# One float32r pass for item 0 ahead of the count, halves, and two PSUM tiles for v in a recurrent scoring kernel

## The chip, the cores and the metric

The kernel runs on one core of a Trainium2 chip. The metric is the device time of one execution in microseconds (us), the median of several. PE is the matmul engine, DVE VectorE, ACT ScalarE, POOL GpSimd, SP SyncE; PSUM is the memory that takes the matmuls' results. Every run is timed beside the kernel before on the same chip.

## The reference, condensed to what matters

```python
emb = emb_table.at[0].set(0.0)              # 100001 x 128
e = emb[seq]                                # 1024 x 50 x 128
prefix = jnp.cumsum(e, axis=1)
uF = prefix / minimum(t + 1, lengths)
y = batchnorm(uF, over the 1024 sequences) * gamma + beta
def step(v, x):                             # 50 steps
    v = v + (x - v) / 2
    spike = v >= 1
    return v - spike, spike
scores = mean(spikes) @ emb.T               # 1024 x 100001, 409.6 MB
```

## The kernel before

Stage one makes 50 steps; stage two multiplies the spike counts with the table and stores the scores. Row 0 of the table (item 0) counts as zeros, but the gathers fetch the row as it is stored; what is called the pass takes it off again. A step of stage one, cut:

```python
# POOL: eight gathers of 128 rows for step t + 1; three tiles e in turn
for n in range(NB):
    nc.gpsimd.indirect_dma_start(out=es[t][:, n * P : (n + 1) * P], ...)
# PE: transposes add the rows to the running sum pre (PSUM)
for n in range(NB):
    nc.tensor.matmul(pre[:, n * P : (n + 1) * P], lhsT=e[...], rhs=ident, is_transpose=True, ...)
for h in range(B // BANK):                      # DVE: statistics
    nc.vector.scalar_tensor_tensor(uF[:, cs], rlen[:, cs], 1.0 / (t + 1), pre[:, cs], ...)
    nc.vector.bn_stats(bs[:, h, :], uF[:, cs])
...
if t:
    spike(t - 1, 0, B)                          # DVE
    nc.vector.tensor_tensor(negv, s, v, ALU.subtract)
    counted(t - 1, s, 0, B)                     # PE, bf16
if not last:
    correct(t + 1, l)                           # PE: "the pass", takes item 0 off pre, FP32
...                                             # DVE: coefficient a
v = ps(2, f"v_{t}")                             # one PSUM tile for v
nc.scalar.activation(v[:, cs], uF[:, cs], AF.Identity, bias=hgb[:, 1:2], scale=a)
nc.vector.scalar_tensor_tensor(v[:, cs], negv[:, cs], -0.5, v[:, cs], ALU.mult, ALU.add)
```

## Time and profile before

| | before |
|---|---|
| timed runs | 1740.95 to 1741.6 us, median 1741.49 |
| the execution that the profile shows | 1716.87 us, span 1715.1 us |
| step of stage one | 11.07 us |
| first store of scores | 591.94 us |
| stage two | 1123 us |

The lines behind this stand in the prediction.

### The profile page before, as it was taken

The page shows a single profiled execution, that of the slowest core. Times are in us where ns is not written, and L with a number is a line of the kernel's source. Part 1 is how long each engine was busy: PE and PEld are TensorE (multiplying, and loading weights), DVE is VectorE, ACT ScalarE, POOL GpSimd, SP SyncE. Part 2 cuts the span into 40 slices and gives each one's busy share as a digit, 9 for nine tenths or more (in the row PEclk, how much of TensorE's full clock was granted, in tenths as well). Part 3 has the DMA queues.
Part 4 walks back from the last instruction along what each step waited for, and adds up shares of the span by engine and source line. Part 5 has one row for each costly group of instructions (what it writes and reads, how often), then busy time and mean ns, then how long its engine had stood idle before and what let it go on. Part 6 is the DMA issues. An engine that isn't in the chain of part 4 may idle for free.

```text
span 1715.1 us, 13957 instructions
## 1 busy us (share of the span) xinstructions
PE 1260.2 (73%) x4614; PEld 837.6 (49%) x4626; DVE 972.8 (57%) x1257; ACT 635.8 (37%) x697; POOL 378.8 (22%) x406
## 2 busy tenths in 40 slices
PE   4555666555565677887788777887778788888886
PEld 1222222222232365665566655666556666666664
DVE  5666666666666644554545545455445555555554
ACT  2222222222222334444434444444344444444443
POOL 7777666766665000000000000000000000000000
PEclk9999999999985589999999999999999999999999
DMA  9811111111111199999999999999999999999998
GB/s 267 241 52 50 47 48 49 48 48 48 47 44 37 71 392 398 395 405 394 387 395 395 401 393 393 394 393 402 393 395 390 397 415 409 403 404 405 403 403 348
DMA packets 97920, 488.71 MB, mean 285 GB/s; under 512 B 14821, under 2 KB 16568, under 8 KB 48696
## 3 DMA queue, kind: packets, MB, share of 16 engines
q1 hardware_dynamic: 85048, 461.59, 69.1%
q0 software_dynamic: 12800, 26.24, 5.4%
q8 instruction: 36, 0.59, 0.1%
q14 instruction: 36, 0.29, 0.1%
HBM read 78.17 MB, written 409.60 MB: 284 GB/s over the span
## 4 chain that ended last, share of the span: by engine, by line
DMA 48%; PE 29%; DVE 18%; ACT 2%; issue 2%; POOL 0%; DVEq 0%; ACTq 0%; SPq 0%
DMA scores<-o 48%; PE pre L175 11%; PE po L295 10%; PE pre L208 5%; DVE o L303 5%; DVE bs L224 4%; DVE uF L221 4%; DVE s L198 3%; PE count L186 3%; ACT o L305 2%; DVE mv L226 1%; PE pt L95 0%; POOL e L125 0%; DVE nm L232 0%; DVE lo L97 0%
## 5 line engine op out<-in xcount | busy, mean ns | idle before, releaser
L295 PE MATMUL po<-hi,countR 128*128 128x512 f32 x1568 | 681.6, 435 | 182.9 <-DVE o L303 181.6
L303 DVE TENSOR_SCALAR o<-po 128x1024 f32<-128x1024 f32 x392 | 479.0, 1222 | 459.7 <-DMA scores<-o 372.0
L295 PE MATMUL po<-lo,countR 128*128 128x512 f32 x1568 | 646.5, 413 | 0.0
L305 ACT ACTIVATE o<-po 128x1024 f32<-128x1024 f32 (+1 forms) x392 | 399.7, 1020 | 633.8 <-DMA scores<-o 394.0
L295 PEld LDWEIGHTS po<-hi,countR 128*128 128x128 f32 x1568 | 314.3, 200 | 341.9 <-DVE o L303 266.9
L125 POOL DMA_INDIRECT e<-in_L_rec_emb_table,idx x400 | 378.1, 945 | 171.5 <-issue 100.7
L295 PEld LDWEIGHTS po<-lo,countR 128*128 128x128 f32 x1568 | 315.3, 201 | 58.3
L186 PE MATMUL count<-s,ident_h 128*128 128x512 bf16 x88 | 45.6, 605 | 225.0 <-DVE s L198 225.0
L175 PE MATMUL pre<-zT,l 50*128 50x512 f32 x200 | 188.9, 1097 | 10.4 <-issue 4.3
L97 DVE TENSOR_TENSOR lo<-pt,hi 128x1024 fp32r<-128x1024 f32 x98 | 119.6, 1221 | 84.8 <-ACT hi L96 84.8
L186 PEld LDWEIGHTS <-ident_h 128*128 128x128 bf16 x100 | 12.6, 126 | 238.0 <-issue 238.0
L230 ACT ACTIVATE r<-mv,eps 128x1 f32<-128x1 f32 x50 | 14.7, 295 | 290.4 <-DVE mv L226 290.4
L221 DVE SCALAR_TENSOR_TENSOR uF<-rlen,pre 128x512 f32<-128x512 f32 x100 | 67.8, 678 | 88.1 <-PE pre L208 88.1
L95 PE MATMUL pt<-ident,rows 128*128 128x128 f32 x782 | 108.2, 282 | 11.2 <-DVE o L303 10.3
L208 PEld LDWEIGHTS pre<-ident,e 128*128 128x128 f32 x400 | 79.0, 224 | 69.2 <-issue 67.7
L95 PEld LDWEIGHTS pt<-ident,rows 128*128 128x128 f32 x782 | 89.4, 144 | 45.3 <-DVE o L303 34.1
L175 PEld LDWEIGHTS pre<-zT,l 50*128 50x128 f32 x200 | 58.3, 321 | 99.0 <-issue 95.2
L96 ACT CAST hi<-pt 128x1024 fp32r<-128x1024 f32 x98 | 98.5, 1005 | 12.0 <-PE pt L95 12.0
L259 ACT ACTIVATE v<-uF,hgb,a 128x1024 f32<-128x1024 f32 (+1 forms) x51 | 60.7, 1190 | 111.4 <-DVE a L251 111.2
L262 DVE SCALAR_TENSOR_TENSOR v<-negv,v 128x1024 f32<-128x1024 f32 (+1 forms) x51 | 61.6, 1208 | 67.5 <-ACT v L259 67.4
L208 PE MATMUL pre<-ident,e 128*128 128x128 f32 x400 | 98.1, 426 | 0.0
L224 DVE BATCH_NORM_STATS2 bs<-uF 128x6 f32<-128x512 f32 x100 | 69.4, 694 | 3.4
(36 smaller groups left out, 284.1 us busy)
## 6 DMA issues: line engine op xcount, KB each, us to landing
scores<-o SPq DMA_DIRECT2D x384, 1024.0 KB, 9.0
scores<-o SPq DMA_DIRECT2D x8, 848.5 KB, 7.4
e<-in_L_rec_emb_table,idx POOLq DMA_INDIRECT x400, 2.5
rows<-in_L_rec_emb_table SPq DMA_DIRECT2D x1, 832.0 KB
rows<-in_L_rec_emb_table SPq DMA_DIRECT2D x48, 0.5 KB, 11.7
len_i<-in_r_lengths SPq DMA_DIRECT2D x1, 512.0 KB, 4.8
idx<-in_r_seq SPq DMA_DIRECT2D x1, 200.0 KB, 2.8
r<-in_L_rec_emb_table SPq DMA_DIRECT2D x1, 25.0 KB
```

What stands on the lines that cost most here:

```text
L95: nc.tensor.transpose(pt[:, k0 : k0 + kw], r[:kw, (h0 + k0) // P, :], ident[:kw, :kw])
L96: nc.scalar.copy(hi[:, :hw], pt[:, :hw])
L97: nc.vector.tensor_tensor(lo[:, :hw], pt[:, :hw], hi[:, :hw].bitcast(F32), ALU.subtract)
L125: nc.gpsimd.indirect_dma_start(out=es[t][:, n * P : (n + 1) * P], out_offset=None, in_=table, in_offset=bass.IndirectOffsetOnAxis(ap=idx[: ...
L175: nc.tensor.matmul(pre[:, h * BANK : (h + 1) * BANK], lhsT=l, rhs=zT[:, h * BANK : (h + 1) * BANK], start=t == 0, stop=False, skip_group_c ...
L186: nc.tensor.matmul(count[:, c : c + BANK], lhsT=ident_h, rhs=s[:, c : c + BANK], start=t == 0, stop=t == T - 1, skip_group_check=True,)
L208: nc.tensor.matmul(pre[:, n * P : (n + 1) * P], lhsT=e[:, n * P : (n + 1) * P], rhs=ident, start=False, stop=last, is_transpose=True, skip ...
L221: nc.vector.scalar_tensor_tensor(uF[:, cs], rlen[:, cs], 1.0 / (t + 1), pre[:, cs], ALU.max, ALU.mult)
L224: nc.vector.bn_stats(bs[:, h, :], uF[:, cs])
L295: nc.tensor.matmul(po[:, k0 : k0 + kw], lhsT=countR[:, n * P : (n + 1) * P], rhs=part[:, k0 : k0 + kw], start=j == 0, stop=j == 1,)
L303: nc.vector.tensor_scalar_mul(o[:, h0 : h0 + hw], po[:, :hw], 1.0 / T)
L305: nc.scalar.mul(o[:, h0 : h0 + hw], po[:, :hw], 1.0 / T)
```

## The change

Its intent: make the pass cheap (one float32r matmul per half, 128 rows deep, the upper rows carrying the remainder of row 0), take it and the count out of the ring of waits, and let DVE work on one half while PE transposes the other. Cut to its core (the preparation of zT and row 0 for the float32r pass, the division of the last step into halves and new pools are left out):

```diff
-            for n in range(NB):
-                nc.tensor.matmul(pre[:, n * P : (n + 1) * P], ..., is_transpose=True)
-            for h in range(B // BANK):
-                nc.vector.scalar_tensor_tensor(uF[:, cs], rlen[:, cs], ..., pre[:, cs], ...)
+            for h, cs in enumerate(halves):
+                for k in range(0, BANK, P):
+                    nc.tensor.matmul(pre[h][:, k : k + P], ..., is_transpose=True)
+                nc.vector.scalar_tensor_tensor(uF[:, cs], rlen[:, cs], ..., pre[h], ...)
                 nc.vector.bn_stats(bs[:, h, :], uF[:, cs])
+            if not last:
+                correct(t + 1, l)
...
             if t:
-                spike(t - 1, 0, B)
-                nc.vector.tensor_tensor(negv, s, v, ALU.subtract)
-                counted(t - 1, s, 0, B)
-            if not last:
-                correct(t + 1, l)
+                if not last:
+                    spike(s, v, whole)
+                for h in range(len(halves)):
+                    counted(t - 1, s, h)
...
-            l = sp.tile([T, D], F32, tag="l", name=f"l_{t}")
+            l = sp.tile([P, D], F32R, tag="l", name=f"l_{t}")
...
-            v = ps(2, f"v_{t}")
+            vt = vp.tile([P, B], F32, tag=f"v{t % 2}", name=f"v_{t}")
```

More of the change, by code (lines that the diff above doesn't have):

```diff
@@ L44, in rec_kernel @@
     NB = B // P
-    assert D == P and B == HALF and T <= P
+    assert D == P and B == HALF and T <= P // 2
     ctx.enter_context(tc.manual_schedule())
     const = ctx.enter_context(tc.tile_pool(name="const", bufs=1))
-    psum = ctx.enter_context(tc.tile_pool(name="psum", bufs=1, space=bass.MemoryType.PSUM))
     embp = ctx.enter_context(tc.tile_pool(name="embT", bufs=4))
     rowp = ctx.enter_context(tc.tile_pool(name="rows", bufs=AHEAD))
-    def ps(i, name):
-        return psum.tile([P, HALF], F32, tag=f"ps{i % 4}", name=name)
     countR = const.tile([P, B], F32R, tag="countR", name="countR")
@@ L77, in fetch, with prepare @@
         rows[c0] = r
-    def prepare(c0, h0, slot):
+    def prepare(c0, h0, pt):
         w = min(CH, N - c0)
@@ L91, in prepare @@
             nc.vector.memset(lo[:, hw : hw + 1].bitcast(F32), 0.0)
-        pt = ps(slot, f"pt_{c0}_{h0}")
         for k0 in range(0, hw, P):
@@ L106, in rec_kernel @@
         lp = ph.enter_context(tc.tile_pool(name="lif", bufs=2))
+        accp = ph.enter_context(tc.tile_pool(name="acc", bufs=1, space=bass.MemoryType.PSUM))
+        vp = ph.enter_context(tc.tile_pool(name="v", bufs=1, space=bass.MemoryType.PSUM))
         idx = once.tile([P, NB, T], I32, tag="idx", name="idx")
@@ L111, in rec_kernel @@
         nc.sync.dma_start(out=len_i, in_=lengths.rearrange("(o b) -> o b", o=1).to_broadcast([P, B]))
-        r0 = once.tile([T, D], F32, tag="r0", name="r0")
-        nc.sync.dma_start(out=r0, in_=table[0:1, :].to_broadcast([T, D]))
+        r0 = once.tile([P, D], F32, tag="r0", name="r0")
+        nc.sync.dma_start(out=r0, in_=table[0:1, :].to_broadcast([P, D]))
         gb = once.tile([P, 2], F32, tag="gb", name="gb")
@@ L135, in rec_kernel @@
         nc.vector.tensor_copy(ident_h, ident)
-        isz = gp.tile([P, NB, T], F32, tag="e", name="isz")
-        nc.vector.tensor_single_scalar(
-            isz.rearrange("p n t -> p (n t)"), idx.rearrange("p n t -> p (n t)"), 0.0, ALU.is_equal
-        )
-        zps = ps(3, "zps")
-        for n in range(NB):
-            nc.tensor.transpose(zps[:T, n * P : (n + 1) * P], isz[:, n, :], ident)
-        zT = once.tile([T, B], F32, tag="zT", name="zT")
-        nc.vector.tensor_copy(zT, zps[:T, :])
-        r0n = once.tile([T, D], F32, tag="r0n", name="r0n")
-        nc.vector.tensor_scalar_mul(r0n, r0, -1.0)
+        isz = gp.tile([P, NB, P], F32, tag="e", name="isz")
+        nc.vector.memset(isz, 0.0)
+        for u in (0, P // 2):
+            nc.vector.tensor_single_scalar(isz[:, :, u : u + T], idx, 0.0, ALU.is_equal)
+        zps = vp.tile([P, B], F32, tag="v1", name="zps")
+        for n in range(NB):
+            nc.tensor.transpose(zps[:, n * P : (n + 1) * P], isz[:, n, :], ident)
+        zT = once.tile([P, B], F32R, tag="zT", name="zT")
+        nc.vector.tensor_copy(zT, zps)
+        r0hi = once.tile([P, D], F32R, tag="r0hi", name="r0hi")
+        nc.scalar.copy(r0hi, r0)
+        r0n = once.tile([P, D], F32, tag="r0n", name="r0n")
+        nc.vector.tensor_scalar_mul(r0n, r0hi.bitcast(F32), -1.0)
+        up2 = slice(P // 2, P)
+        nc.vector.tensor_tensor(r0n[up2, :], r0hi[up2, :].bitcast(F32), r0[up2, :], ALU.subtract)
+        sel = once.tile([P, P // 2], F32, tag="sel", name="sel")
+        nc.vector.tensor_tensor(sel, ident[:, : P // 2], ident[:, P // 2 :], ALU.add)
         rlen = once.tile([P, B], F32, tag="rlen", name="rlen")
@@ L161, in rec_kernel @@
         nc.vector.memset(negv, 0.0)
-        pre = ps(0, "pre")
-        count = ps(1, "count")
+        pre = [accp.tile([P, BANK], F32, tag=f"pre{h}", name=f"pre{h}") for h in range(B // BANK)]
+        count = [accp.tile([P, BANK], F32, tag=f"count{h}", name=f"count{h}") for h in range(B // BANK)]
         def row0(t):
-            l = sp.tile([T, D], F32, tag="l", name=f"l_{t}")
-            nc.scalar.activation(l, r0n, AF.Copy, scale=ident[:T, t : t + 1])
+            l = sp.tile([P, D], F32R, tag="l", name=f"l_{t}")
+            nc.scalar.activation(l, r0n, AF.Copy, scale=sel[:, t : t + 1])
             return l
@@ L175, in correct @@
                 nc.tensor.matmul(
-                    pre[:, h * BANK : (h + 1) * BANK],
+                    pre[h],
                     lhsT=l,
@@ L182, in correct, with counted, spike @@
                 )
-        def counted(t, s, b0, b1):
-            for c in range(b0, b1, BANK):
-                nc.tensor.matmul(
-                    count[:, c : c + BANK],
-                    lhsT=ident_h,
-                    rhs=s[:, c : c + BANK],
-                    start=t == 0,
-                    stop=t == T - 1,
-                    skip_group_check=True,
-                )
+        def counted(t, s, h):
+            nc.tensor.matmul(
+                count[h],
+                lhsT=ident_h,
+                rhs=s[:, h * BANK : (h + 1) * BANK],
+                start=t == 0,
+                stop=t == T - 1,
+                skip_group_check=True,
+            )
+        def spike(s, v, cs):
+            nc.vector.tensor_single_scalar(s[:, cs], v[:, cs], V_TH, ALU.is_ge)
+        whole = slice(0, B)
+        halves = [slice(h * BANK, (h + 1) * BANK) for h in range(B // BANK)]
         v = s = None
-        def spike(t, b0, b1):
-            nc.vector.tensor_single_scalar(s[:, b0:b1], v[:, b0:b1], V_TH, ALU.is_ge)
         correct(0, row0(0))
@@ L206, in rec_kernel @@
             e = es.pop(t)
-            for n in range(NB):
-                nc.tensor.matmul(
-                    pre[:, n * P : (n + 1) * P],
-                    lhsT=e[:, n * P : (n + 1) * P],
-                    rhs=ident,
-                    start=False,
-                    stop=last,
-                    is_transpose=True,
-                    skip_group_check=True,
-                )
+            if last:
+                spike(s, v, whole)
+                nc.vector.tensor_tensor(negv, s, v, ALU.subtract)
             uF = up.tile([P, B], F32, tag="uF", name=f"uF_{t}")
             bs = sp.tile([P, B // BANK, 6], F32, tag="bs", name=f"bs_{t}")
-            for h in range(B // BANK):
-                cs = slice(h * BANK, (h + 1) * BANK)
-                nc.vector.scalar_tensor_tensor(
-                    uF[:, cs], rlen[:, cs], 1.0 / (t + 1), pre[:, cs], ALU.max, ALU.mult
-                )
+            for h, cs in enumerate(halves):
+                for k in range(0, BANK, P):
+                    nc.tensor.matmul(
+                        pre[h][:, k : k + P],
+                        lhsT=e[:, h * BANK + k : h * BANK + k + P],
+                        rhs=ident,
+                        start=False,
+                        stop=last,
+                        is_transpose=True,
+                        skip_group_check=True,
+                    )
+                nc.vector.scalar_tensor_tensor(uF[:, cs], rlen[:, cs], 1.0 / (t + 1), pre[h], ALU.max, ALU.mult)
                 nc.vector.bn_stats(bs[:, h, :], uF[:, cs])
+            if not last:
+                correct(t + 1, l)
             mv = sp.tile([P, 2], F32, tag="mv", name=f"mv_{t}")
@@ L238, in rec_kernel @@
             if t:
-                spike(t - 1, 0, B)
-                nc.vector.tensor_tensor(negv, s, v, ALU.subtract)
-                counted(t - 1, s, 0, B)
-            if not last:
-                correct(t + 1, l)
+                if not last:
+                    spike(s, v, whole)
+                for h in range(len(halves)):
+                    counted(t - 1, s, h)
             nc.vector.reciprocal(r, r)
@@ L251, in rec_kernel @@
             nc.vector.tensor_scalar(a, r, hgb[:, 0:1], None, ALU.mult)
-            v = ps(2, f"v_{t}")
-            s = lp.tile([P, B], BF16, tag="s", name=f"s_{t}")
-            step = BANK if last else B
-            for b0 in range(0, B, step):
-                cs = slice(b0, b0 + step)
-                nc.scalar.activation(v[:, cs], uF[:, cs], AF.Identity, bias=hgb[:, 1:2], scale=a)
-            for b0 in range(0, B, step):
-                cs = slice(b0, b0 + step)
-                nc.vector.scalar_tensor_tensor(v[:, cs], negv[:, cs], -0.5, v[:, cs], ALU.mult, ALU.add)
-                if last:
-                    spike(t, b0, b0 + step)
-                    counted(t, s, b0, b0 + step)
+            vt = vp.tile([P, B], F32, tag=f"v{t % 2}", name=f"v_{t}")
@@ new lines, in rec_kernel @@
+            st = lp.tile([P, B], BF16, tag="s", name=f"s_{t}")
+            for h, cs in enumerate(halves if last else [whole]):
+                nc.scalar.activation(vt[:, cs], uF[:, cs], AF.Identity, bias=hgb[:, 1:2], scale=a)
+                if t and not last:
+                    nc.vector.tensor_tensor(negv, s, v, ALU.subtract)
+                nc.vector.scalar_tensor_tensor(vt[:, cs], negv[:, cs], -0.5, vt[:, cs], ALU.mult, ALU.add)
+                if last:
+                    spike(st, vt, cs)
+                    counted(t, st, h)
+                    for k in range(0, BANK, P):
+                        put = nc.scalar.copy if k % (2 * P) == 0 else nc.vector.tensor_copy
+                        put(countR[:, h * BANK + k : h * BANK + k + P], count[h][:, k : k + P])
@@ L266, in rec_kernel @@
+            v, s = vt, st
             if t + 2 < T:
                 l = row0(t + 2)
-            if T - 8 <= t < T - 4:
-                prepare((t - T + 8) // 2 * CH, t % 2 * HALF, 3)
-        for n in range(NB):
-            cs = slice(n * P, (n + 1) * P)
-            if n % 2 == 0:
-                nc.scalar.copy(countR[:, cs], count[:, cs])
-            else:
-                nc.vector.tensor_copy(countR[:, cs], count[:, cs])
+            if T - 10 <= t < T - 2 and t % 2 == 0:
+                k = (t - T + 10) // 2
+                prepare(k // 2 * CH, k % 2 * HALF, vp.tile([P, HALF], F32, tag="v1", name=f"pt_{k}"))
@@ L280, in rec_kernel @@
     op = ctx.enter_context(tc.tile_pool(name="o", bufs=4, reuse_waits="tile"))
-    turn = slot = 0
+    psum = ctx.enter_context(
+        tc.tile_pool(name="psum", bufs=4, space=bass.MemoryType.PSUM, reuse_waits="tile")
+    )
+    turn = 0
     for c0 in range(0, N, CH):
@@ L288, in rec_kernel @@
                 hw = min(HALF, w - h0)
-                po = ps(slot, f"po_{c0}_{n}_{h0}")
-                slot += 1
+                po = psum.tile([P, HALF], F32, tag="ps", name=f"po_{c0}_{n}_{h0}")
                 for k0 in range(0, hw, BANK):
@@ L311, in rec_kernel @@
                 if nxt + h0 < N:
-                    prepare(nxt, h0, slot)
-                    slot += 1
+                    prepare(nxt, h0, psum.tile([P, HALF], F32, tag="ps", name=f"pt_{nxt}_{h0}"))
             if n == 4 and c0 + AHEAD * CH < N:
```

## The prediction

> **What bounds the kernel now.** I read the page's slices first, then the windows, then one step of the first stage in the chain of waits and the timeline, and last the waits of the engine that seemed unimportant. In the slices the DMA share is 1 tenth from the third slice to the fourteenth and 9 tenths after it, so there are two stages. In the timeline the first store of scores is issued at 591.94 us and the span ends at 1715.1 us. The windows (start:end, length, then busy time of PE, PEld, DVE, ACT, POOL; granted clock, DMA share, GB/s) show what each stage is short of:
>
> ```profile
> 200.00:300.00 100.00, 59.11 (x126) 26.75 (x126) 67.01 (x136) 25.81 (x36) 67.90 (x72) 1.00 0.17 48
> 300.00:400.00 100.00, 58.87 (x124) 26.75 (x126) 67.29 (x136) 25.81 (x36) 68.24 (x73) 1.00 0.17 48
> ...
> 700.00:1715.00 1015.00, 830.09 (x3502) 609.05 (x3502) 529.29 (x441) 437.14 (x439) 0.00 (x0) 0.95 1.00 396
> ```
>
> Stage two is DMA at a share of 1.00 and 396 GB/s. The change does not alter its bytes, so I take its 1715.1 - 591.9 = 1123 us as fixed: what matters is when the first store leaves. In stage one no engine is busy over 70%, so it must be a chain, here one step of it (start, us, what):
>
> ```profile
> 302.63 0.22 DVE mv L226
> 302.88 0.15 DVE nm L232
> 303.03 0.06 DVE ve L235
> 303.10 1.14 DVE s L198
> 304.24 0.04 issue
> 304.28 1.01 PE count L186 x2
> 305.29 3.71 PE pre L175 x4
> 309.00 1.92 PE pre L208 x8
> 310.94 0.70 DVE uF L221
> ```
>
> The reader is to see a ring: statistics (2.8 us), aggregation, spike, count, the 3.71 us pass that takes item 0 off, eight transposes, and again statistics at 310.94. The one before began at 299.87: a step is 11.07 us. The pass sits behind the count in PE's order, the count behind the spike; so PE's 6.7 us lie in series with 4.4 us of DVE. The timeline shows DVE idle 1.99 us before each uF, waiting for the transposes.
>
> The reader should also look at POOL, which gathers the embeddings, eight gathers in a step:
>
> ```profile
> 304.28 0.10 PEld L186 LDWEIGHTS <-ident_h 128*128 128x128 bf16 x1 [4.72 <-issue]
> 305.11 0.94 POOL L125 DMA_INDIRECT e<-in_L_rec_emb_table,idx  x1 [0.30 <-issue]
> ...
> 306.36 0.94 POOL L125 DMA_INDIRECT e<-in_L_rec_emb_table,idx  x1 [0.31 <-issue]
> ...
> 307.61 0.95 POOL L125 DMA_INDIRECT e<-in_L_rec_emb_table,idx  x1 [0.30 <-issue]
> ```
>
> ```profile
> POOL e L125 <- issue: 100.7, 330, 0.6
> POOL e L125 <- PE pre L208: 58.3, 39, 3.7
> ```
>
> They start 1.25 us apart, 0.94 us of work and a gap of 0.30 us for which nothing is named (330 times). Eight are 10.0 us of the 11.07. The remaining wait, 58.3 us in 39 steps, is for a gather buffer that the transposes free. POOL's 68% busy hides an engine that can go at most 10% faster: the gap belongs to its period.
>
> [...] four FP32 instructions over 512 columns are 3.71 us for both halves, against a start distance of 0.43 us for a float32r matmul of 512 columns at the start of stage two (586 to 592 us)[...]. [...] here 0.944 us stand against a median of 2.5 us from issue to landing. [...] the gathers last 938/944/1438 ns (least/median/most), one of them at 1.44 us in the prologue and otherwise steady beside a DVE that is 67% busy[...].
>
> **The change, part by part.** (1) The pass becomes one float32r matmul for each half, 128 rows deep (upper rows carry the remainder of row 0): 2 x 0.43 = 0.9 us, call it 1.1 with its loads, so 2.6 us less PE work. (2) It moves in front of the count and needs only the uF operations that read its half, so PE does transposes, pass, count, and then the next step's transposes without waiting for DVE's later work: the order of instructions of the changed kernel shows this, each transpose waiting only for its own gather. PE's 1.97 + 1.1 + 1.0 = 4.1 us leave the ring. (3) With two PSUM tiles for v, the subtraction for negv (1.2 us) moves from before the coefficient a to the time in which ACT computes v (1.21 us). DVE's chain then is, with starts read from the step at 299.87: statistics, aggregation and spike 4.39 us; reciprocal to a, 1.04 us; ACT's v with negv beside it, 1.26 us; the update of v, 1.25 us; together 7.9 to 8.0 us. If DVE set the pace, 11.07 would become 8.0.
>
> (4) It does not: the gathers need 8 x 1.25 = 10.0 us in a step. POOL begins at 3.78 us and is not held in front: its third tile needs the first transposes, which by my count end at about 23.5 us (zeroed isz tile, two comparisons and the split of row 0 delay the prologue by some 2 us, the shorter pass gives 2.7 back), while POOL comes to it at 25.0. Step t of DVE would start at 28.5 + 8t, its last gather lands at about 16 + 10t; from t = 6 on POOL sets the pace. In the trace before, the 33rd gather starts at 44.98; 367 more at 1.25 give 503.7, plus 2.5 for landing 506.2 us.
>
> (5) The end: one transpose and the second half's uF and bn (about 508.4; the first half waits for spike and negv of the step before, which costs half a us), aggregation 0.25, coefficient 1.4, first half of v on ACT 0.8, update, spike 1.4, count 0.6, four copies of 0.31 to countR, then update, spike, count of the second half 2.0: 516.2 us for the first product, for which the two counts stand ahead on PE. Before it was 586.52. The 5.4 us from there to the first store stay, so 521.6 against 591.9: 70 us less. Of these some 53 are the pace (50 x 1.07), 9 the four prepared tiles (2.2 us of each was in the ring, now in POOL's shadow, as 8.0 + 1.7 is under 10), the rest the prologue that POOL has already overlapped and the shorter end. Stage two is unchanged but for its pool of four PSUM tiles, used in the same turn.
>
> Timed runs are longer than the profiled span (1741.49 against 1715.1); I take the 26 us over. 1741.5 - 70.3 = 1671 us, 4.0% less.
>
> **The rivals.** (a) DVE sets the pace and the gathers keep up: 50 x 8.0 + 28.5 + 12 would put the first store near 445, some 147 us less, 1594 us. For it, POOL looks only 68% busy; against it, the gap of 0.30 us appears 330 times, also in the first 25 us where no buffer is awaited. I think this the trap in the change. (b) The ring closes elsewhere: the transposes of the tile being prepared need a v tile, v must wait for it, and DVE waits on copies in the last step. At 3 us for each of four tiles 12 us are lost: 1683 us. [...] (d) The time saved is lost in stage two: it would need under 373 GB/s instead of 396; nothing in the diff does that.
>
> **Range and chances.** POOL's rate is measured on 400 instructions, and 0.02 us on the period is 8 us; prologue and end are good to 5 us; (b) and (c) lie above, and only (a) below. So 1658 to 1688 us, eight times in ten. Faster by 2% means under 1706.7 us, half of my gain: 0.95. Within 2%: 0.04. Slower: 0.01.
>
> **What would show it right or wrong.** Right: steps 10.0 us apart; POOL's wait for the transposes gone and its starts 1.25 us apart to the end; PE or DVE waiting for gathers in most steps; the pass at 0.4 to 0.6 us for each half; DVE about 80% busy in the middle of the stage; the last gather at about 504 us; first store at about 522; 1123 us after it. A step of 8 us would mean that the gap of 0.30 us is not part of POOL's period; over 10.3, that a wait that I have not seen entered the ring; a first store at 522 without the gain, that stage two was slowed.

The forecast's sum is 1741.5 - 70.3 = 1671 us. Rival (c): a denser DVE slows the gathers, by a guessed share. The paragraph before "The change, part by part" compares measured times: the pass's four FP32 records are 3.71 us, matmuls of float32r in a row start 0.43 us apart (at a granted clock of 0.50, `--windows 586:592`), and a gather's record is 0.944 us where it lands after 2.5.

## The result, and the profile after

The changed kernel took 1725.22 us (1723.19 to 1726.24, four runs) against 1741.22 us of the kernel before in the same rounds. The ratio is 0.9907, 95% interval 0.9889 to 0.9924: the same within 2%. I had expected 0.96.

The windows of its profiled execution (1723.19 us), in the columns that the prediction explains:

```profile
200.00:300.00 100.00, 36.65 (x104) 21.76 (x104) 64.58 (x134) 24.89 (x36) 67.14 (x71) 0.53 0.16 47
...
700.00:1640.00 940.00, 776.91 (x3269) 576.02 (x3267) 492.78 (x409) 409.46 (x409) 0.00 (x0) 0.94 1.01 398
```

Stage two is as before (share 1.01, 398 GB/s). In stage one POOL makes 71 gathers in 100 us where before it made 72, and the granted clock (third number from the end) has fallen from 1.00 to 0.53. The first store leaves at 598.5 us, later than the 591.94 of before. The chain of waits shows where the time is (start, us, what):

```profile
112.69 1.12 DVE negv L266
...
114.02 1.23 DVE v L267
115.25 7.52 another core or an unknown queue
122.77 0.02 issue
122.79 0.69 DVE uF L228
...
124.21 2.85 another core or an unknown queue
127.06 0.69 DVE uF L228
```

DVE is done at 115.25 and waits 7.5 us and then 2.9 us for something that the profile cannot name. Such a stall comes in every third step: the other two take 7.74 us, the third 18.3, together 33.8 us or 11.27 us a step (the mean of steps 10 to 40). POOL's waits (line, releaser: us in total, times, longest) and the statistics' group:

```profile
POOL e L122 <- issue: 109.3, 358, 0.6
POOL e L122 <- remote: 64.4, 16, 5.4
```

```profile
L228 DVE SCALAR_TENSOR_TENSOR uF<-rlen,pre 128x512 f32<-128x512 f32 x100 | 67.9, 679 | 144.8 <-remote 129.3 <-issue 14.7 <-PE pre L219 0.7
```

POOL's wait for the transposes (58.3 us before) is gone by name, but 64.4 us of "remote", in 16 waits, stand in its place; DVE's wait before uF is "remote" as well. This is a kernel on one core: nothing remote exists in it. The timeline around the stall (start, us, instruction, in brackets the idle time before it):

```profile
112.60 1.91 PE L219 MATMUL pre<-ident,e 128*128 128x128 f32 x8
...
122.79 0.69 DVE L228 SCALAR_TENSOR_TENSOR uF<-rlen,pre 128x512 f32<-128x512 f32 x1 [7.54 <-remote]
...
127.05 0.69 DVE L228 SCALAR_TENSOR_TENSOR uF<-rlen,pre 128x512 f32<-128x512 f32 x1 [2.84 <-remote]
127.29 0.95 POOL L122 DMA_INDIRECT e<-in_L_rec_emb_table,idx  x1 [4.09 <-remote]
```

The eight transposes that DVE and POOL wait for start at 112.60 and look finished at 114.51. The records of PE's semaphore updates say otherwise. These are us after the step's first transpose, read from the trace: the first number of the stalled step is the count's update, the next eight are the transposes'.

```
stalled step, at 112.60:  0.36 | 2.46 5.26 7.36 10.17 12.96 14.36 14.40 14.43
prompt step,  at 130.95:  0.22 | 0.43 0.64 0.86 1.07 (two missing) 1.71 1.92
```

The fourth transpose's update comes at 122.77, and uF starts at 122.79; the eighth comes at 127.03, and the second uF starts at 127.05. So these late updates are what everybody waited for. Their gaps are multiples of 0.70 us (2.10, 2.80, 2.10, 2.81, 2.79, 1.40), and the last three arrive 0.03 us apart, faster than PE can transpose (its starts are 0.21 us apart). Hence PE had done the work, and the news of it was late. Only PE's news was: in the same stretch a VectorE update is recorded at 127.75, 0.01 us after its uF ends, and updates of gathers' transfers are recorded at 114.46, 115.73 and 116.94, some 2.2 us after those gathers start. Whether PE's writes to PSUM were still awaited or only the updates were held up, the trace does not say. The rows were there too: the last packet of this step's gathers ends at 104.40 us. The matmuls' records do not show this: the eight look finished at 114.51, and the last update comes at 127.03, 12.5 us later.

In this trace many records of semaphore updates are missing altogether, while the records of instructions are not (13874, against 13863 in the control below). One sign stands on the page, in the issues of transfers, whose last number should be the time from issue to landing; there is none:

```profile
e<-in_L_rec_emb_table,idx POOLq DMA_INDIRECT x400
```

### The profile page after: what moved, and what is told of

Its sections match the earlier page's. It is cut to its first block, busy times and chain, and to the rows that moved or that the text cites. A ratio compares the mean times of both kernels' runs of the same rounds, so it can differ in the third digit from the quotient of the medians.

```text
span 1721.3 us, 13874 instructions
## 1 busy us (share of the span) xinstructions
PE 1141.8 (66%) x4526; PEld 820.3 (48%) x4526; DVE 969.4 (56%) x1261; ACT 636.3 (37%) x698; POOL 379.5 (22%) x406
## 4 chain that ended last, share of the span: by engine, by line
DMA 48%; DVE 23%; PE 10%; another core or an unknown queue 9%; ACT 5%; issue 4%; POOL 0%; ACTq 0%; DVEq 0%; SPq 0%
DMA scores<-o 48%; PE po L301 9%; DVE bs L229 4%; ACT o L311 4%; DVE uF L228 4%; DVE v L267 3%; DVE s L199 3%; DVE negv L266 2%; DVE o L309 2%; ACT v L264 1%; DVE mv L233 1%; DVE a L257 1%; DVE r L255 1%; DVE q L254 0%
## 5 line engine op out<-in xcount | busy, mean ns | idle before, releaser
L179 PE MATMUL pre<-zT,l 128*128 128x512 f32 x100 | 72.7, 729 | 264.4 <-DVE uF L228 196.0
L179 PEld LDWEIGHTS pre<-zT,l 128*128 128x128 f32 x100 | 27.0, 271 | 306.0 <-issue 192.2
L189 PE MATMUL count<-s,ident_h 128*128 128x512 bf16 x100 | 50.7, 608 | 88.9 <-DVE s L199 67.8
L91 ACT CAST hi<-pt 128x1024 fp32r<-128x1024 f32 x98 | 98.5, 1005 | 16.1 <-remote 11.3
L219 PEld LDWEIGHTS pre<-ident,e 128*128 128x128 f32 x400 | 86.7, 228 | 21.3 <-issue 18.6
```

The lines of the kernel that those rows point to most:

```text
L91: nc.scalar.copy(hi[:, :hw], pt[:, :hw])
L179: nc.tensor.matmul(pre[h], lhsT=l, rhs=zT[:, h * BANK : (h + 1) * BANK], start=t == 0, stop=False, skip_group_check=True,)
L219: nc.tensor.matmul(pre[h][:, k : k + P], lhsT=e[:, h * BANK + k : h * BANK + k + P], rhs=ident, start=False, stop=last, is_transpose=True, ...
```

## The experiments

Theory A: the pass now waits for two engines (uF from DVE, l from ACT), PE executes a separate wait instruction in front of it (49 EVENT_SEMAPHORE records of 51 ns at its line, against one in the kernel before), and this delays its updates. Theory B: PE, 37% busy instead of 59%, is granted half its clock (the link between the two is part of the theory), and that makes its updates late. Theory D was added after the first four runs: the stalls belong to the chip. Theory N: the path of the semaphore updates and their records is what is narrow there. Runs with a ratio were timed in three rounds and their fast runs compared; the others (c2, e6 to e14, c3) are single profiled executions of unknown state, so differences of a few us between them carry nothing.

### Four edits (chip 11)

l_on_vector, so that the pass waits for DVE alone:

```diff
-            nc.scalar.activation(l, r0n, AF.Copy, scale=sel[:, t : t + 1])
+            nc.vector.tensor_scalar(l, r0n, sel[:, t : t + 1], None, ALU.mult)
```

> The kernel after, with one edit: the small operand l of the pass is made by VectorE instead of ScalarE, so that the first matmul of the pass waits for one engine's semaphore and not for two[...]. Theory A (that stand-alone wait of PE delays the completions of its own transposes in every third step): the stalls of about 7.5 us before the first half of uF vanish, steps are 10.0 us apart (8 gathers of 1.25 us), the last gather starts near 504 us, time 1670 to 1680 us. Theory B (PE, less busy than before, is granted half its clock, and its completions come late because of that): nothing changes, clock 0.5 through stage one, three steps in 33.8 us, 1722 to 1727 us. VectorE does 0.1 to 0.2 us more in a step, which lies beside the gathers under A.

dummy, eight matmuls of zeros behind the transposes, so that PE stays busy:

```diff
+            if t > 1:
+                for i in range(8):
+                    nc.tensor.matmul(count[i % 2], lhsT=ident_h, rhs=zero, start=False, stop=False, ...)
             if not last:
                 correct(t + 1, l)
```

> The kernel after, with eight matmuls of zeros into the count added behind the transposes of each step (correct result), so that PE is about as busy as before. Theory B (the lower granted clock makes the completions late): the clock of stage one goes back to 1.0 as in the kernel before, the stalls of every third step vanish, steps 10.0 us apart, 1670 to 1685 us. Theory A (the two-semaphore wait): the clock goes to 1.0 but the stalls stay, 1720 to 1730 us. If the clock stays at 0.5 the run tells nothing of B.

order_only, the kernel before with its FP32 pass moved:

```diff
+            if not last:
+                correct(t + 1, l)
             mv = sp.tile([P, 2], F32, tag="mv", name=f"mv_{t}")
...
                 counted(t - 1, s, 0, B)
-            if not last:
-                correct(t + 1, l)
```

> The kernel before with one edit: the pass[...] is put in front of the count. PE stays as busy as before and gets the wait for two engines in front of the pass. Theory A: stalls of several us appear in every third step, no faster than the kernel before, 1725 to 1745 us. Theory B: clock 1.0, no stalls, and as about 2 us of the count leave the ring of waits, the step falls from 11.07 to 10.0 us (the gathers' floor): 1670 to 1690 us.

pass_only, the kernel before with the float32r pass in the old place (the preparation of zT and row 0 that goes with it is left out here):

```diff
-            l = sp.tile([T, D], F32, tag="l", name=f"l_{t}")
-            nc.scalar.activation(l, r0n, AF.Copy, scale=ident[:T, t : t + 1])
+            l = sp.tile([P, D], F32R, tag="l", name=f"l_{t}")
+            nc.scalar.activation(l, r0n, AF.Copy, scale=sel[:, t : t + 1])
```

> The kernel before with one edit: the pass is one float32r pass[...], still behind the count, so that no new wait on two engines arises. Theory A: no stalls, ring of about 11.07 less 2 to 3 us, so the gathers' floor of 10.0 us per step: 1670 to 1685 us at whatever clock. Theory B: PE is less busy, the clock falls to 0.5 in stage one, and stalls of every third step appear: 1720 to 1745 us.

| run | us | ratio, 95% | step, us |
|---|---|---|---|
| e1_l_on_vector | 1645.39 | 0.9586 [0.9570, 0.9602] | 9.99 |
| e2_dummy | 1646.0 | 0.9590 [0.9574, 0.9606] | 10.01 |
| e3_order_only | 1651.42 | 0.9623 [0.9607, 0.9639] | 9.98 |
| e4_pass_only | 1649.87 | 0.9613 [0.9597, 0.9629] | 10.00 |

No run stalled: not order_only, in which A wanted stalls, not l_on_vector and pass_only, which ran at a clock of 0.50 and 0.56 (100 to 400 us) and in which B wanted them. The first half of B fails as well: order_only, with all of the kernel before's PE work in shorter steps (422 matmuls in 300 us against 374, PE 69% busy), was granted 0.52, where the kernel before at 59% had 1.00. What sets the clock stays open. And the kernel before took 1716.73 us beside them, not 1741. So all four "cures" worked, which means that none of them was one. A control was missing.

### The control: the changed kernel again

> The kernel after, unchanged: a control. The four edits of the first series all ran without stalls, even those that theory A or theory B alone would have left stalled, and the kernel before took 1716.7 us there, not the 1741.2 us of the rounds in which after was first timed. Theory A or B (the stalls belong to the kernel after, and each edit happened to remove them): stalls again in every third step, 1722 to 1727 us. Theory D (the stalls belong to the chip, or to the session, on which the rounds of after ran, and not to the change): no stalls here, about 1645 us beside a kernel before of about 1717 us, ratio near 0.958; or, if it comes to a chip of the other kind, about 1725 beside 1741 again.

It took 1645.16 us beside 1717.13 us (chip 6), ratio 0.9582 [0.9566, 0.9598]: 4.2% faster, with no edit. Its windows and POOL's waits:

```profile
200.00:300.00 100.00, 49.65 (x119) 23.36 (x121) 73.88 (x152) 28.69 (x40) 75.62 (x81) 0.50 0.20 53
...
700.00:1640.00 940.00, 784.74 (x3262) 589.24 (x3262) 492.36 (x412) 407.06 (x409) 0.00 (x0) 0.91 1.00 398
```

```profile
POOL e L122 <- issue: 117.2, 385, 0.3
...
POOL e L122 <- PE pre L219: 1.5, 5, 0.3
```

POOL makes 81 gathers in 100 us, at the same granted clock of 0.5; "remote" is gone, and the wait for the transposes is 1.5 us in all. The chain of waits now runs through POOL:

```profile
301.91 0.94 POOL e L122
302.85 0.30 issue
303.15 0.94 POOL e L122
304.10 0.30 issue
304.40 2.42 DMA e<-in_L_rec_emb_table,idx
```

The reader sees the predicted period of 1.25 us (301.91 to 303.15), with the unnamed 0.30 us in it. The landing time is back on the page, at the predicted 2.5 us:

```profile
e<-in_L_rec_emb_table,idx POOLq DMA_INDIRECT x400, 2.5
```

The same program, instruction for instruction, thus takes 1725 or 1645 us. A and B fall as causes that lie in the kernel. The run was repeated later, beside the one with more transfers below:

> The kernel after, unchanged, once more, as the last run came to a chip on which the kernel before took 1746.8 us. Theory D or N: if the kernel before beside it takes 1740 us or more, stalls of 14 us again in every third step or so, 1720 to 1730 us, update records missing and PE's completions in steps of 0.70 us; if before takes 1717 us, none of it and 1645 us. A stalled run beside a before of 1717, or a clean one beside a before of 1741, would refute both.

1644.42 us beside 1717.34 us, steps of 9.99 us, chip 6 again: D's second branch, as expected.

### What each part gives on such a chip

halves_only: the changed kernel with the old FP32 pass behind the count (its old preparation is left out here).

```diff
-            l = sp.tile([P, D], F32R, tag="l", name=f"l_{t}")
+            l = sp.tile([T, D], F32, tag="l", name=f"l_{t}")
...
-            if not last:
-                correct(t + 1, l)
             mv = sp.tile([P, 2], F32, tag="mv", name=f"mv_{t}")
...
                     counted(t - 1, s, h)
+            if not last:
+                correct(t + 1, l)
```

> The kernel after with the old pass put back:[...] behind the count; so only the halves and the two PSUM tiles for v are left of the change. On the two chips of the runs so far the kernel before takes 1717 us and steps are 11.07 us apart. My own step (3) says that the ring here is: statistics of the second half, aggregation, spike, count and pass (4.7 us of PE behind the spike), transposes of the first half, then again statistics; with 2 us of transposes now half hidden, 11.07 less about 1 to 1.4 us (the second half's transposes run beside uF of the first half), so 9.7 to 10.0, and the gathers' 10.0 us set the pace: 1645 to 1655 us, steps 10.0 us apart. If the halves hide nothing: about 1712 to 1717 us, 11 us. On a chip of the kind on which after was first timed (before 1741 us): stalls of several us in every third step or so, and more than 1700 us.

It took 1675.97 us beside 1716.51 us (chip 12), ratio 0.9763 [0.9747, 0.9779], steps of 10.21 us. My 1645 to 1655 us was a miss. The step is near what I said, but it is a ring still, its chain (start, us, what) runs through the FP32 pass:

```profile
301.91 1.14 DVE s L193
303.05 0.04 issue
303.10 0.58 PE count L183
303.68 0.36 issue
304.04 3.78 PE pre L173 x4
307.82 1.06 PE pre L213 x4
```

and its first product comes at 545.9 us, 30 us behind the 515.4 of the changed kernel in the control. By step 40 it is 19 us behind (431.4 against 412.5): its steps are 10.2 us from the second on, while the changed kernel starts with 7.7 to 9.7 us until the gathers set its pace. Another 12 us come from four steps of 13.25 us, in which the prepared tiles stand in the ring. So the pass alone or its place alone brings 65 to 67 us, the halves alone 40, all together 72. They do not add up because the gathers set a floor that each of the first two reaches.

few_gathers: four gathers in a step, the other blocks read the first four again. Its output is wrong, which doesn't matter for the time. Once for each kernel (the kernel before has `e[:, n % 4 * P : ...]` in the place of the last line):

```diff
-            for n in range(NB):
+            for n in range(NB // 2):
                 nc.gpsimd.indirect_dma_start(
...
-                        lhsT=e[:, h * BANK + k : h * BANK + k + P],
+                        lhsT=e[:, k : k + P],
```

> The kernel after, wrong on purpose: only four of the eight gathers of a step are made, and the transposes of the other four blocks read the first four again. Everything else is as in after. If the gathers set the pace on an undisturbed chip (step (4) of the prediction), the step falls from 10.0 us to the chain of VectorE and ScalarE, 7.7 to 8.0 us (predicted 7.9 to 8.0, seen as 7.74 between the stalls), POOL waits for the transposes in every step, and the time is about 1645 less 50 times 2.1 to 2.3 us: 1530 to 1545 us. If something else than the gathers' rate holds the step at 10 us, it stays there and so does the time. On a chip of the kind on which after was first timed: half the gathers, half the semaphore increments of the transfers; if those increments or their records are what delays PE's completions, the stalls go away or get rarer there too; if they come from PE alone, they stay, at 14 us each.

> The kernel before with the same edit. The ring of PE and VectorE sets its pace and not the gathers, so the step stays at 11.0 to 11.1 us and the time within 10 us of the kernel before beside it (the prologue may be a few us shorter). If gathers had a part in its 11.07 us, it gets faster by more than 20 us.

After: 1558.59 us, steps of 7.72 us (over the expected 1530 to 1545: the pace was right, but the four steps with a prepared tile take 10.6 to 12.3 us once no gather hides them). Before: 1712.09 us, steps of 11.06 us. Before 1716.68 us, chip 11. POOL's first wait, of the changed kernel with four gathers:

```profile
POOL e L122 <- PE pre L219: 154.0, 46, 7.5
```

So on this chip the gathers, and nothing else, hold the changed kernel at 10 us; they have no part in the 11.07 us of before. DVE's chain is 7.72 us.

### The other kind of chip

more_records: the changed kernel, with tiny transfers in every step, each of which adds 16 semaphore increments (as a gather does: the first profile of before has 800 landing updates for 50 gathers on each of eight semaphores; three tiny transfers show 48 in a full step of e9).

```diff
             nc.vector.tensor_scalar_add(ve, mv[:, 1:2], BN_EPS)
+            scr = sp.tile([16, 24], F32, tag="scr", name=f"scr_{t}")
+            for i in range(24):
+                nc.sync.dma_start(out=scr[:, i : i + 1], in_=ve[:16, :])
```

> The kernel after, with 24 tiny transfers (16 numbers each, from the statistics of the step to a scratch tile) issued by SyncE in every step; the result stays correct. Each transfer adds 16 semaphore increments, so the trace should hold some 50 semaphore updates per us in stage one where after has 15.7. Theory N: what delayed PE's completions in the first run of after is the path that carries semaphore updates and their records, overrun on that chip; many of the update records are missing there (3.7 per us recorded instead of 15.7). If that path is the weak spot, a load three times as high brings the same signs on an undisturbed chip: missing records, PE completions some us late, stalls of POOL for no named reason, well over 1660 us. If the path has ample room, nothing happens: steps 10.0 us apart, 1645 to 1655 us; then N is not supported as a matter of load, and the stalls stay a property of that chip or that moment.

> The kernel with 24 tiny transfers in a step, unchanged, as a control of the run that took 1965.7 us with steps of 15.3 us on a chip with a before of 1746.8 us. Beside a before of 1717 us, theory N (the path of the records is narrow on some chips only): the tiny transfers cost at most what SyncE needs to issue them and wait for them[...]; steps 10.0 to 10.5 us, all update records there (50 per us), 1645 to 1670 us. If the 15.3 us are simply what 24 such transfers take, steps are about 15 us here too and the run before it says nothing of the chip.

The first came to chip 10, where the kernel before took 1746.83 us: 1965.68 us, steps of 15.27 us. The second came to chip 6, before 1717.34 us: 1963.25 us, steps of 15.26 us. My estimate of what the transfers cost, hidden by the gathers' 10 us, was wrong by far; the 15.3 us are simply their price, on either chip: SyncE issues one every 0.63 us, and 24 take 15.2. As a stress of the update path the pair still says something. Semaphore updates recorded per us, from 100 to 400 us and, for comparison, from 700 to 1000 us, counted in the traces of all the runs concerned:

```
kernel                        before beside it   100-400 us   700-1000 us
before (first profile)        1717 (itself)         14.1           7.6
before (c3)                   1746                   5.1           7.6
after (c1)                    1717                  15.7           7.6
after (first run)             1741                   3.7           7.6
pass and order (e10)          1745                   3.7           7.7
four gathers (e6)             1717                  11.1           7.6
four gathers (e11)            1746                   9.8           7.6
24 transfers (e9)             1717                  32.9          (17.7)
24 transfers (e8)             1747                  12.6          (13.9)
```

(In brackets: stage one reaches to 800 us there.) Where before takes 1717 us, the load of e9 makes no update of PE late. But its records are not complete: 512 of its updates in a step come from transfers (24 x 16 tiny ones, 8 x 16 of gathers), 33.6 per us in steps of 15.26 us, and the trace holds 30.9 of them (in a full step 48 for three tiny transfers, in others down to 19). So missing records alone don't make late updates. Where it takes 1741 to 1747 us, records are missing in stage one of every kernel. Yet N in its simple form, too many updates per us, fails: e8 makes as many updates as e9 in steps of the same length, and in its steady steps PE's updates come 0.22, 0.43 ... 1.93 us after the start, prompt. It stalls only at its beginning: before its first tiny transfer is issued at 69.1 us, VectorE stands idle before uF for 8.2 us in the second step and 9.1 us in the third, after the transposes' records have ended; e9 has neither.

pass_and_order: the kernel before with both edits on the pass, without halves and with one tile for v (the diffs of e3 and e4 together).

> The kernel before with the float32r pass and with it in front of the count, so after without its halves and without the second PSUM tile for v. Beside a before of 1717 us: the gathers set the pace already, steps 10.0 us, and only the end (5 us, the last step undivided) is left to gain: 1648 to 1652 us. If pass and order together leave less slack than each alone, or the halves are needed for the pace, over 1655 us. Beside a before of 1740 us or more (a chip of the other kind): stalls as in the first run of after, missing update records, 1720 to 1735 us; if the stalls belong to the halves, they are not there.

It came to chip 0, before 1745.05 us: 1730.39 us, and stalls in every third step: 8.99, 8.98 and 16.1 us, 11.35 on average. In its chain:

```profile
111.69 7.01 another core or an unknown queue
118.70 0.02 issue
118.72 0.70 DVE uF L227
```

So the stalls need neither halves nor two v tiles. And two kernels whose own chains are 7.74 and 8.99 us end at nearly the same average. That suggested a rate for the eight gathers of a step. Two runs together, the kernel with four gathers unchanged and the kernel before unchanged:

> The kernel after with four gathers in a step (wrong on purpose) took 1558.6 us beside a before of 1716.7 us, steps 7.72 us, PE's completions prompt. Wanted is this kernel on a chip where before takes 1740 us or more. Two kernels there (after, and pass and order alone) kept an average of 11.3 us per step whatever their own chain was (7.74 and 8.99 us), as if 8 gathers could not be carried faster than in 11.3 us, 1.41 us each. If the limit is on what a gather brings with it (its landing, its semaphore increments, their records), four gathers need 5.6 us, less than the chain's 7.72: no stalls, 1555 to 1570 us. If the limit is PE's or the step's own, stalls remain and the average step stays above 10 us, over 1670 us. On a chip with a before of 1717 us: 1558 us again, which tells nothing.

> The kernel before, unchanged, for a trace of it beside the one above. On a chip where it takes 1740 us or more: are its 25 us more spent in the same way, with PE's completions late in some steps and update records missing (theory D or N: yes, some steps of 14 us or more among steps of 11.07 us, average about 11.6 us, stage two as ever at 1123 us)? If its steps are all alike, or the loss is in stage two, the two kernels do not suffer from the same thing. On a chip of 1717 us: steps of 11.07 us, nothing new.

They came to chip 10, before 1745.86 us. Four gathers: 1558.92 us (1558.59 on chip 11), steps of 7.72 us, PE's updates prompt, no stall. The limit does not belong to PE's work of a step, which is the same as in the stalling kernel. The kernel before: 1745.42 us, its steps 11.06, 11.06, 11.06 and then one of about 12.5, on average 11.41 us, first store at 620.2 us, 28 us later than in the first profile, 1123 us after it. POOL's waits in it:

```profile
POOL e L125 <- PE pre L208: 75.9, 43, 3.7
POOL e L125 <- remote: 11.8, 3, 5.8
```

It suffers from the same thing, but its own ring of 11.07 us is only some 0.3 us shorter than a step at the limit, so that it loses little: 50 x 0.34 = 17 us in the pace, and 12 us in one stall of its third step.

In the four traces with eight gathers that stall (after, e8, e10, c3) the limit is not there from the start: the 32nd gather starts at 43.4 to 43.9 us, as in the control (43.5), and the 48th at 68.6 to 69.7 us (63.5 in the control). So something can run ahead for some 32 to 40 gathers before it stalls; what that is, these runs do not show.

six_gathers: the same edit with six gathers, three times, as I could not choose the chip.

```diff
-            for n in range(NB):
+            for n in range(6):
                 nc.gpsimd.indirect_dma_start(
...
+                    b = (h * BANK + k) % (6 * P)
...
-                        lhsT=e[:, h * BANK + k : h * BANK + k + P],
+                        lhsT=e[:, b : b + P],
```

> The kernel after with six gathers in a step instead of eight (wrong on purpose, the last two blocks read the first two again). On a chip with a before of 1717 us: six gathers need 7.5 us, just under the chain's 7.72, so steps of 7.7 to 7.9 us and 1558 to 1570 us. On a chip with a before of 1740 us or more, if what the chip limits is the gathers, at 1.41 to 1.43 us each (11.27 to 11.40 us for eight in three kernels there): six need 8.5 us, so some steps with late completions, an average step of 8.4 to 8.6 us and 1595 to 1610 us. If the limit there is a matter of a whole step (11.3 us or nothing), or of all eight gathers, the average is 7.7 or 11.3 us.

> Six gathers in a step again, as the last run came to a chip with a before of 1716.3 us and took 1561.7 us there. On a chip with a before of 1740 us or more: 8.4 to 8.6 us as the average step and 1595 to 1610 us if the limit is 1.41 to 1.43 us for each gather; 7.7 us and 1562 us if six gathers are as free as four; about 11.3 us and over 1690 us if the limit belongs to the step. On a chip of 1716 us it repeats and tells nothing.

> The last try of six gathers in a step, the two before having met chips with a before of 1716 us. Same expectations: beside a before of 1740 us or more 8.4 to 8.6 us per step and 1595 to 1610 us under a limit of 1.41 to 1.43 us for each gather, 7.7 us and 1562 us if six are as free as four, over 1690 us if the limit belongs to the step.

All three met chips of the first kind (1, 11 and 12; before 1716.3, 1716.41 and 1717.42 us): 1561.73, 1562.28 and 1561.79 us, steps of 7.79 us. On those chips six gathers are as good as hidden. The question they were sent for stays open.

### What is shown and what is open

Shown: chips 11 (three visits), 6 and 12 (two each) and 1 let the kernel before run in 1716 to 1717 us, chips 10 (two visits) and 0 in 1745 to 1747; no chip changed its kind. On the second kind, kernels with eight gathers in a step do not go below 11.27 to 11.41 us a step on average (after, pass and order, before), four gathers run free at 7.72 us, and a kernel with eight gathers in 15.3 us has prompt updates in its steady steps. The stall itself is PE's semaphore updates arriving up to 12.5 us late, with update records missing: the traces of kernels that make about 14 semaphore updates per us (15.7 x 9.99 / 11.27 = 13.9, an estimate) kept only 3.7 to 5.1 of them on the second kind, while a chip of the first kind kept 32.9 of about 35.5 (estimated from 512 updates of transfers and some 30 of engines in 15.26 us). Whether the kind belongs to the chip itself or to something else at work beside the kernel there is not tested: only chip 10 of the second kind was visited twice. That the first rounds of the changed kernel (before 1741.22 us) met this second kind is an inference from the time of before, the 0.70 us quantum, which e10 shows too (its updates come 2.30, 5.10, 7.21, 9.33 and 10.74 us into a stalled step), and the missing records; the result of that run names no chip.

Open: the mechanism. Where PE's updates come late, records of updates are missing too (3.7 per us recorded against 15.7), but that the two have one cause is not shown: e8, with 12.6 recorded against 32.9 in e9, does not stall in its steady steps, and every run here is recorded, so that I could not take the recording away. Whether the rate is one for each gather (11.3 / 8 = 1.41 us, an estimate) is open as well.

A version that beats both kernels by more did not come out of this: the changed kernel is the faster one on both kinds of chip (by 4.2% on the first, by 0.9% in the first rounds), and on the first kind POOL, with one instruction for each 128 rows, is its floor (8 x 1.25 = 10.0 us a step).

## Why the prediction was right or wrong, point by point

- **Stage two fixed at 1123 us: right.** 1122.8 us in the first run (1721.3 - 598.5), 1122.7 in the control (1643.2 - 520.5).
- **Step (1), the pass: mis-sized, without effect.** A half's record is 0.73 to 0.76 us, not 0.4 to 0.6; my 0.43 us was the distance of starts in a row, and a record is longer: 0.79 us for the first of that row, 0.63 for the next ones. The granted clock is no reason, it was 0.50 there and 0.50 to 0.53 here. e2_dummy, at 0.72 of the clock from 100 to 400 us, gains nothing.
- **Steps (2) and (3), the ring and DVE's chain: right.** 7.74 us between stalls and 7.72 us with four gathers, against 7.9 to 8.0.
- **Step (4), the gathers set the pace: right on the first kind of chip.** Steps of 9.99 us, last gather at 502.9 us (503.7 predicted). On the chip of the timing this step failed, with what it rests on, 8 x 1.25 = 10.0 us: gathers still start 1.25 us apart, but PE's late updates hold POOL 64.4 us in all, and eight cost 11.27 us.
- **Step (5), the end: right.** First product at 515.41 us (516.2), first store at 520.5 (521.6). The gain in the control is 1717.13 - 1645.16 = 72.0 us against 70.3.
- **"Timed runs are longer than the profiled span (1741.49 against 1715.1); I take the 26 us over": this is the step that failed.** Only 1.8 us of it are the difference between a span and its run. The other 24.6 us said that the timed runs did not go as the profiled one did. c3 shows what they are: steps that average 11.41 instead of 11.07 us, and a first store 28 us later. They are no constant to be carried over, but a limit that shows with eight gathers in a step, of which the kernel before feels little and the changed one much: its first store comes 598.5 - 520.5 = 78 us later. On the first kind of chip the same step failed the other way: the control's 1645.2 us lie 26 us under the forecast 1671, because no 26 us were there to be carried.
- **The rivals.** (a) would have needed gathers that keep up; only with four of them does DVE set the pace (7.72 us), and nearly so with six (7.79). Its sum is 440.5, not "near 445"; nothing hangs on that. (b) is real where no gather hides it (10.6 to 12.3 us steps in e6), but is hidden with eight. (c) is dead: a gather takes 947 ns in the first run and 945 in the control, where before it took 945. (d) is dead with the first point. None of mine asked whether profile and times came from the same conditions.
- **Of the signs that I named**, 81 gathers in 100 us and waits of PE for gathers (121.3 us before the transposes in the control) came true there; DVE at about 80% was 74%. In the first run "over 10.3, a wait that I have not seen entered the ring" came true.

## What to carry to other kernels

Before a profile is used to predict a time, hold the profiled execution's own time against the timed runs: where they differ by more than the runs among themselves, they come from different conditions, and the difference may be the very limit that the change will meet. When every edit cures a fault, rerun the unedited kernel before believing any of them. Where an engine's record has ended and everybody still waits for it, look at its semaphore updates (12.5 us late here) and not at its busy time.
